# Issuing a second pass's gathers behind the third feed-forward pair's weight sums, and one weight product in another place, on one core

## The chip, the cores and the metric

One core of one Trainium2 chip runs the whole program. The metric is the device time of one execution in microseconds (us); lower is better. The engines are called PE (TensorE matmul), PEld (its weight loads), DVE (VectorE), ACT (ScalarE), POOL (GpSimd) and SP (SyncE).

## The reference

The input x has 32 sequences of 64 tokens, 1024 wide, in float32. One transformer block is computed:

- a linear layer with a low-rank addition chosen by a label for each sequence (`x @ W.T + 0.5 * (x @ A[label]) @ B.T`, rank 32, 5 labels),
- attention on its result (32 query heads, 8 key and value heads, rotary embedding, causal softmax, output projection), added to x,
- a linear layer with a mixture of 8 low-rank experts (top 2 after a bias for the language of the sequence),
- a feed-forward linear layer with a second mixture of 8 low-rank experts, whose result is added again.

No nonlinear function stands between the first linear layer and the query, key and value projection, nor between the third and the fourth layer. The kernel therefore multiplies the weights of such neighbours with each other first.

## The kernel before

**Stages.** Stage 1 multiplies weights: `cq` (first layer by the query and key columns), `ckv` (by the rest of the keys and the values) and `cf` (third layer by fourth). Their results go to scratch in HBM (`cqkv`, `cffn`, `wos`). Stage 2 is run twice, for `hf` 0 and 1, each with 16 of the 32 sequences: low-rank rows, query and key products (`qk_pair`), scores, softmax, values, output projection (`o_pairs`), router gates, and four feed-forward pairs (`ffn_pair(0)` to `ffn_pair(3)`, called f00 to f03 in the first pass below).

**Seven products in place of eight.** Every large product is cut into 2 by 2 blocks and done with seven block products and some sums (class `Group`). Its steps `p1` to `p7` are block products of 4 chunks each; they accumulate in three PSUM banks x, y and z:

- x takes `p1`, and then `p2` on top; `out00` reads it.
- y takes `p6`, then `p7`, then `p4`. Between them DVE reads it: after `p6` for `add01` (line 285, tile `cq_u` or `f_u`), after `p7` for `add11` (line 297), after `p4` for `out10`.
- z takes `p5`, then `p3`. Between them `out11` reads it, which needs `add11` too; after `p3`, `out01` reads it.

A later step of a bank waits on PE until the earlier reader is through. The banks come from `group_bank`, three in turn, so that the sixth bank taken is the third one again, once it has been read.

**Weight sums.** `weight_sums` makes four 128x512 sums of a weight tile on POOL (lines 176 to 179). Tiles `w` and `s` have two buffers each, so the sums of the third pair wait until the first pair's last product with a sum, `p3`, is done.

**Stage 1 order.** SP, PE and DVE follow the order written in the code. For `cq` the first two groups are interleaved by hand, in the list `order` of the call of `multiply`; a step `(1, "p5")` is `p5` of group 1.

**First feed-forward pair.** Its main products run before its gates are there (`without_extra`). Then `scaled` turns the gates round on PE (`gpr`), copies them on ACT (`gsr`) and multiplies on DVE (`hwr`), and `with_extra` adds the expert terms (line 270) to z, x and y, calls `out11` and `out00`, and goes on with `p3` and `out10`. The other pairs use `Group.main`, with the expert terms as a fifth chunk of each product (`tail`, line 265).

**Gathers.** For each sequence `gathered` issues one indirect DMA on POOL's queue, which fetches 128 rows of the label's low-rank factor. For the first pass they are issued in stage 1, in two lots of eight. For the second pass all 16 go into a part of tile `q`, and the place in POOL's queue is set by hand:

```python
with tc.issue_after(late["gates"].ins):
    tiles = [
        gathered(hf, s, lambda name: a1[:, s * BS : (s + 1) * BS], BS) for s in range(NS)
    ]
```

`late["gates"]` is the last copy made by `gates_of`, on POOL at line 756: at that point the first pass's second gates. The gathered rows are first used by `first_halves`, at the head of the second pass's PE work.

Of the kernel before, what the change touches and what calls it, by code (L numbers as in the profile page):

```python
# [13 lines left out]
F32 = mybir.dt.float32  # L14
# [5 lines left out]
P = 128  # L20
D = 1024
KC = D // P
# [3 lines left out]
E, R = 8, 16  # L26
# [3 lines left out]
NT = TH // P  # L30
# [46 lines left out]
def block_kernel(ctx: ExitStack, tc: tile.TileContext, a, out: bass.AP):  # L77
    nc = tc.nc
    PSUM = bass.MemoryType.PSUM

    const = ctx.enter_context(tc.tile_pool(name="const", bufs=1))
# [13 lines left out]
    def tmp(name):  # L95
        return tp.tile([P, 512], F32, tag="t", name=name)

    def small(name):
        return sm.tile([P, NT, E], F32, tag="small", name=name, bufs=12)


    cst = const.tile([P, NCONST], F32, tag="consts", name="consts")
    ident, parts = cst[:, _C["ident"]], cst[:, _C["parts"]]
    stack = cst[:, _C["stack"]]
# [64 lines left out]
    def weight_sums(w, name, s=None):  # L169

        h = w.shape[1] // 2
        a11, a12 = w[:, :h, :P], w[:, h:, :P]
        a21, a22 = w[:, :h, P:], w[:, h:, P:]
        if s is None:
            s = wp.tile([P, 4, h, P], F32, tag="s", name=f"s_{name}")
        nc.gpsimd.tensor_add(s[:, 0], a21, a22)  # L176
        nc.gpsimd.tensor_sub(s[:, 1], s[:, 0], a11)
        nc.gpsimd.tensor_sub(s[:, 2], a11, a21)
        nc.gpsimd.tensor_sub(s[:, 3], a12, s[:, 1])
        return s  # L180

    def column_sums(t, b, cols, which=range(4)):
# [216 lines left out]
    def load_w(from_, name):  # L399
        w = wp.tile([P, KC, WG], F32, tag="w", name=f"w_{name}")  # L400
        nc.sync.dma_start(w, from_)
        return w
# [6 lines left out]
    def gathered(hf, s, new, n):  # L409

        tiles = []
        for b0 in range(0, BS, n):
            t = new(f"a1_{hf}_{s}_{b0}")
            for b in range(n):
                at = hf * BH + s * BS + b0 + b
                nc.gpsimd.indirect_dma_start(
                    t[:, b, :],
                    None,
                    a["a1"],
                    bass.IndirectOffsetOnAxis(ap=rows_of[:, at : at + 1], axis=0),  # L420
                )
            tiles.append(t)
        return tiles

    def ranks(hf, s, x, tiles, low):

        n = BS // len(tiles)
        ps = ps_tile(f"h_{hf}_{s}")
        rows = tmp(f"rows_{hf}_{s}")

        def half(i):
            for b in range(BS):
                for g in range(4):
                    kc = i * 4 + g
                    nc.tensor.matmul(
                        ps[g * LR : (g + 1) * LR, b * S : (b + 1) * S],
                        tiles[b // n][:, b % n, kc * LR : (kc + 1) * LR],
                        x[kc][:, (s * BS + b) * S : (s * BS + b + 1) * S],

                        start=(i, b) == (0, 0),  # L440
                        stop=i == 1,
                        skip_group_check=True,
                    )
            if i == 1:

                nc.scalar.mul(rows, ps, 0.5)

        def stacked():
            ps = ps_tile(f"low_{hf}_{s}")
            nc.tensor.matmul(ps, stack, rows, start=True, stop=True)  # L450
            nc.scalar.copy(low[:, s * 512 : (s + 1) * 512], ps)

        return lambda: half(0), lambda: half(1), stacked

    def new_low(hf):
        return hp.tile([P, TH], F32, tag="hw", name=f"low_{hf}")
# [22 lines left out]
    with tc.tile_pool(name="gen", bufs=1) as gen:  # L479
# [146 lines left out]
        def load_kv(w):  # L626
# [4 lines left out]
            "cq", "w1", t_cq, D, cqkv, 0, first=(w0, w1),  # L631
            order=[
                *((0, "p1"), (1, "p1"), (0, "p2"), (1, "p2"), (0, "p6"), (0, "p5"), (0, "p7"), (1, "p6")),
                *((0, "out11"), (0, "p4"), (0, "p3"), (1, "p5"), (1, "p7"), (1, "out11"), (1, "p4"), (1, "p3")),
            ],
            after={
                (0, "p1"): lambda w: b1q_rows[0](),
# [63 lines left out]
        )  # L701


    late = {"logits": const.tile([P, KC, 32], F32, tag="wr", name="wr")}
    nc.sync.dma_start(late["logits"], a["wr2"])
    in_order.close()

# [3 lines left out]
    def gates_of(n, hf, lgv, more):  # L711


        nm = f"r{n}_{hf}"

        def wide(v):
            return v.unsqueeze(2).to_broadcast([P, NT, E])

        def one(name):
            return sm.tile([P, NT], F32, tag="one", name=f"{name}{nm}", bufs=10)  # L720

        em = em8.unsqueeze(1).to_broadcast([P, NT, E])
        l1 = small(f"l1{nm}")
        nc.vector.tensor_add(l1, lgv, more)

        def first_max(lv, k):

            m = one(f"m{k}")
            nc.vector.tensor_reduce(m, lv, AX.X, ALU.max)
            eq = small(f"eq{k}{nm}")  # L730
            nc.vector.tensor_tensor(eq, lv, wide(m), ALU.is_equal)
            nc.vector.tensor_mul(eq, eq, em)
            i = one(f"i{k}")
            nc.vector.tensor_reduce(i, eq, AX.X, ALU.min)
            oh = small(f"oh{k}{nm}")
            nc.vector.tensor_tensor(oh, em, wide(i), ALU.is_equal)
            return m, oh

        m1, oh1 = first_max(l1, 1)
        l2 = small(f"l2{nm}")  # L740
        nc.vector.scalar_tensor_tensor(l2, oh1, -3e38, l1, ALU.mult, ALU.add)
        m2, oh2 = first_max(l2, 2)

        e = one("e")
        nc.vector.tensor_sub(e, m2, m1)
        nc.scalar.activation(e, e, AF.Exp)
        g1 = one("g1")
        nc.vector.tensor_scalar(g1, e, 0.5, 0.5, ALU.mult, ALU.add)
        nc.vector.reciprocal(g1, g1)
        g2 = one("g2")  # L750
        nc.vector.tensor_mul(g2, g1, e)
        nc.vector.tensor_mul(oh1, oh1, wide(g1))
        nc.vector.tensor_mul(oh2, oh2, wide(g2))
        nc.vector.tensor_add(oh1, oh1, oh2)
        gates = late["pool"].tile([P, NT, E, R], F32, tag="gates", name=f"gates{nm}")
        late["gates"] = nc.gpsimd.tensor_copy(gates, oh1.unsqueeze(3).to_broadcast([P, NT, E, R]))
        return gates

    def scaled(n, hf, h, gates):
# [17 lines left out]
    def scoped(name, bufs=1, side="left"):  # L777
        return pools.enter_context(tc.tile_pool(name=name, bufs=bufs, side=side, reuse_waits="tile"))

    for hf in range(2):  # L780
# [13 lines left out]
        if hf == 0:  # L794
            low = first_pass["low"]
        else:

            low = new_low(hf)
            a1 = q[:, 1].rearrange("p b m t -> p b (m t)")
            with tc.issue_after(late["gates"].ins):  # L800
                tiles = [
                    gathered(hf, s, lambda name: a1[:, s * BS : (s + 1) * BS], BS) for s in range(NS)
                ]
            steps = [ranks(hf, s, x, tiles[s], low) for s in range(NS)]
            first_halves, second_halves, sums = zip(*steps)
# [248 lines left out]
        with tc.manual_schedule():  # L1054
# [3 lines left out]
            for u in range(2):  # L1058
                g = pair
# [26 lines left out]
            sums = scoped(f"sums_o{hf}")  # L1086
# [141 lines left out]
        def ffn_pair(g):  # L1228
            w = load_w(cffn[:, :, g * WG : (g + 1) * WG], f"f{hf}{g}")

            def out_f(r, c, ps, add):
                oc = 2 * g + r
                o = tmp(f"o_{hf}_{oc}_{c}")
                if add is None:
                    nc.scalar.activation(o, ps, AF.Identity, bias=bb[:, oc : oc + 1])
                else:
                    nc.vector.scalar_tensor_tensor(o, ps, bb[:, oc : oc + 1], add, ALU.add, ALU.add)  # L1237
                nc.scalar.dma_start(out[oc, :, hf, c, :], o)

            def extra(r, c):  # L1240
                if (r, c) == (0, 1):
                    return [(bd[:, 0], hw2[1]), (bd[:, 1], hw3[1])]
                return [(b2v[:, 0, r], hw2[c]), (b3v[:, 0, r], hw3[c])]

            def tail(left, right):
                lhs = {"11": b2v[:, g, 0], "12": b3v[:, g, 0], "22": b3v[:, g, 1]}
                rhs = {"11": hw2[0], "21": hw3[0], "22": hw3[1]}
                return (
                    bs[:, int(left[1]) - 1, g - 1] if left[0] == "s" else lhs[left],
                    th[:, int(right[1]) - 1] if right[0] == "t" else rhs[right],  # L1250
                )

            s = weight_sums(w, f"f{hf}{g}")
            if g == 0:
                return Group(f"f{hf}{g}", w, s, xt, out_f, extra, late=True)
            group = Group(f"f{hf}{g}", w, s, xt, out_f)
            group.tail = tail
            return group
# [19 lines left out]
        first.with_extra()  # L1278
        column_sums([th[:, j] for j in range(4)], lambda i, c: (hw2, hw3)[i][c], lambda t: t)
        for g in range(1, 4):  # L1280
            ffn_pair(g).main()
        pools.close()


# [86 lines left out]
```

## Time and profile before

| | |
|---|---|
| median of 3 runs | 1216.33 us (1215.64 to 1218.25) |
| the profiled execution's own time | 1218.22 us |
| its span, first to last instruction | 1216.5 us, granted TensorE clock 0.998 |
| PE busy | 1204.8 us (99%) |
| DVE, POOL, ACT busy | 582.2, 509.6, 153.6 us |
| DMA | 108.83 MB, mean 89 GB/s |
| the second pass's 16 gathers on POOL | from 633.83 to 654.11 us |
| second pass's first use of the gathered rows | 753.25 us |

Times in the views are us from the span's start. A timeline row has start, duration, engine, line, operation, tiles and count; in brackets stands the idle time of the engine before it, and what ended it. "remote" there means that a semaphore moved which the profile can lay to no instruction that had just ended. A row of the view by stretches has the stretch, its length, the busy time of PE, PEld, DVE, ACT and POOL with the number of instructions, the granted PE clock, the DMA engines' busy share and GB/s.

### The profile page before, as it was taken

To read this page: it belongs to the slowest core of one execution; us is meant where nothing else is said; L and a number is where in the kernel's file an instruction comes from. 1 tells how busy PE (TensorE), PEld (TensorE's weight loads), DVE (VectorE), ACT (ScalarE), POOL (GpSimd) and SP (SyncE) were. 2 spreads that over 40 slices of the span, in tenths; PEclk is the share of its full clock that TensorE was granted. 3 is DMA by queue.
4 is the path that set the end of the run, shared out by engine and by line. 5 is a ranking of instruction groups with operands and counts; after the bars stand their busy time and mean duration, and the time that the engine had idled before them with its cause. 6 is when DMAs were issued, how large, how long until landed. Compare 5 with 4: busy or idle time off the path is not lost.

```text
span 1216.5 us, 13619 instructions
## 1 busy us (share of the span) xinstructions
PE 1204.8 (99%) x5440; PEld 612.9 (50%) x5440; DVE 582.2 (48%) x941; ACT 153.6 (13%) x282; POOL 509.6 (42%) x437
## 2 busy tenths in 40 slices
PE   9999999999999999999998999999999999999998
PEld 3444875555444477544443444444468544444443
DVE  5212161115358789764832113456789764842111
ACT  1001000000001125320000000100214330000000
POOL 3441351443435746745635011542756653821010
PEclk9999999999999999999999999999999999999999
DMA  6653732644111111122114225111120123112110
GB/s 243 222 205 110 273 120 81 205 146 153 35 34 36 43 62 71 43 74 96 35 47 126 69 85 192 36 35 35 36 70 17 55 70 116 60 35 69 57 48 34
DMA packets 58992, 108.83 MB, mean 89 GB/s; under 512 B 5168, under 2 KB 35248, under 8 KB 57648
## 3 DMA queue, kind: packets, MB, share of 16 engines
q1 hardware_dynamic: 43136, 79.53, 19.7%
q10 hardware_dynamic: 13104, 20.03, 4.5%
q0 software_dynamic: 2688, 8.39, 2.1%
q8 instruction: 43, 0.70, 0.3%
q14 instruction: 21, 0.17, 0.0%
HBM read 83.72 MB, written 24.22 MB: 89 GB/s over the span
## 4 chain that ended last, share of the span: by engine, by line
PE 97%; DMA 1%; DVE 0%; another core or an unknown queue 0%; SPq 0%; ACT 0%; issue 0%; DVEq 0%; ACTq 0%
PE qk_y L255 9%; PE o_y L255 7%; PE f_y L255 7%; PE qk_x L255 6%; PE qk_z L255 6%; PE v L873 5%; PE f_z L255 5%; PE o_x L255 5%; PE f_x L255 5%; PE o_z L255 5%; PE cq_y L255 3%; PE cf_y L255 3%; PE sc L894 3%; PE pt L947 2%; PE cf_z L255 2%; PE cq_z L255 2%
## 5 line engine op out<-in xcount | busy, mean ns | idle before, releaser
L823 POOL TENSOR_TENSOR raw<-raw,consts 128x512 f32<-128x512 f32 x40 | 63.1, 1586 | 105.8 <-DVE t L822 105.8
L927 POOL TENSOR_TENSOR e<-e,top 128x512 f32<-128x512 f32 x64 | 65.0, 1045 | 57.3 <-DVE top L926 42.2
L939 POOL TENSOR_TENSOR e<-e,tot 128x512 f32<-128x512 f32 x64 | 66.2, 1067 | 27.2 <-DVE tot L937 27.2
L255 PE MATMUL qk_x<-x,w_qk 128*128 128x512 f32 x160 | 72.2, 594 | 0.0
L255 PE MATMUL qk_y<-sum_x,s_qk 128*128 128x512 f32 x160 | 72.2, 594 | 0.0
L176 POOL TENSOR_TENSOR s_f<-w_f 128x512 f32<-128x512 f32 x8 | 11.0, 1370 | 127.6 <-DMA w_f<-cffn 99.7
L255 PE MATMUL o_x<-q,w_o 128*128 128x512 f32 x128 | 58.9, 592 | 0.0
L873 PE MATMUL v<-w_v,x 128*128 128x256 f32 x256 | 58.7, 382 | 0.0
L255 PE MATMUL f_x<-x,w_f 128*128 128x512 f32 x128 | 57.9, 592 | 0.0
L255 PE MATMUL f_y<-sum_y,s_f 128*128 128x512 f32 x128 | 57.5, 592 | 0.0
L1048 POOL TENSOR_TENSOR x<-x,o_u 128x512 f32<-128x512 f32 x24 | 31.0, 1294 | 54.2 <-DVE o_u L1046 33.2
L873 PEld LDWEIGHTS v<-w_v,x 128*128 128x128 f32 x256 | 47.4, 190 | 8.4 <-issue 2.7
L255 PEld LDWEIGHTS qk_x<-x,w_qk 128*128 128x128 f32 x160 | 30.1, 190 | 38.0 <-issue 37.9
L824 DVE TENSOR_TENSOR t<-t,consts 128x512 f32<-128x512 f32 x40 | 48.7, 1230 | 0.7
L255 PEld LDWEIGHTS qk_y<-sum_x,s_qk 128*128 128x128 f32 x160 | 30.2, 190 | 37.1 <-issue 36.6
L176 POOL TENSOR_TENSOR s_qk<-w_qk 128x512 f32<-128x512 f32 x10 | 19.1, 1906 | 65.8 <-DMA w_qk<-cqkv 65.8
L936 DVE TENSOR_REDUCE tot<-e 128x8 f32<-128x512 f32 x64 | 40.5, 666 | 10.7 <-ACT e L931 10.4
L931 ACT ACTIVATE e<-e 128x512 f32<-128x512 f32 x64 | 38.2, 639 | 54.3 <-POOL e L927 54.2
L917 DVE TENSOR_TENSOR e<-sc,consts 128x512 f32<-128x512 f32 x64 | 39.7, 676 | 8.8 <-PE sc L894 8.8
L1237 DVE SCALAR_TENSOR_TENSOR o<-f_z,consts,f_u 128x512 f32<-128x512 f32 x16 | 12.0, 751 | 58.6 <-PE f_z L265 42.6
L255 PEld LDWEIGHTS f_y<-sum_y,s_f 128*128 128x128 f32 x128 | 24.3, 190 | 30.6 <-issue 30.6
L255 PEld LDWEIGHTS f_x<-x,w_f 128*128 128x128 f32 x128 | 24.3, 190 | 30.6 <-issue 30.6
(321 smaller groups left out, 2239.3 us busy)
## 6 DMA issues: line engine op xcount, KB each, us to landing
w_qk<-cqkv SPq DMA_DIRECT2D x10, 1024.0 KB, 6.2
x<-in_xT SPq DMA_DIRECT2D x16, 512.0 KB, 8.1
w_o<-in_wo SPq DMA_DIRECT2D x16, 512.0 KB, 4.9
s_o<-wos SPq DMA_DIRECT2D x16, 512.0 KB, 6.7
w_f<-cffn SPq DMA_DIRECT2D x8, 1024.0 KB, 5.4
outT<-o ACTq DMA_DIRECT2D x32, 256.0 KB, 2.8
cqkv<-cq ACTq DMA_DIRECT2D x16, 256.0 KB, 2.3
w_ckv<-in_w SPq DMA_DIRECT2D x4, 1024.0 KB, 6.6
```

The costliest lines, as they stand in the source:

```text
L176: nc.gpsimd.tensor_add(s[:, 0], a21, a22)
L255: nc.tensor.matmul(ps, self.weights[left][:, kc, :], self.right(right, kc), start=first and kc == 0, stop=kc == self.h - 1, skip_group_che ...
L823: nc.gpsimd.tensor_mul(rv, rv, c3)
L824: nc.vector.tensor_mul(t2v, t2v, s3)
L873: nc.tensor.matmul(begun[t], x[kc][:, t * P : (t + 1) * P], wv[:, kc, :], start=False, stop=kc == KC - 1, skip_group_check=True,)
L894: nc.tensor.matmul(sc[j][:, n * S : (n + 1) * S], q[rows, g, b, 2 * mp : 2 * mp + 2, :].rearrange("p m t -> p (m t)"), k[rows, g, b, :], s ...
L917: nc.vector.tensor_add(per_key(e), per_key(sc[j]), mask.unsqueeze(1).to_broadcast([P, 8, S]))
L927: nc.gpsimd.tensor_sub(ev, ev, wide(top))
L931: nc.scalar.activation(e, e, AF.Exp, scale=SCALE)
L936: nc.vector.tensor_reduce(tot[:, i], es[i], AX.X, ALU.add)
L939: nc.gpsimd.tensor_mul(es[i], es[i], wide(tot[:, i]))
L1048: nc.gpsimd.tensor_add(xo, xo, to)
```

## The change

Two edits. In the first, each call of `weight_sums` keeps its last instruction in `late["sums"]`, the one of the third pair (`g == 2`) is kept as `late["third"]`, and the second pass's gathers are issued after it; nothing is kept of the gates any more. POOL's queue then holds the second gates' copy, the four sums `s_f02`, the 16 gathers, the four sums `s_f03`; before it held the copy, the gathers, `s_f02`, `s_f03`. In the second, `(0, "p3")` of the `cq` list moves from behind `(0, "p4")` to behind `(1, "p7")`. The queue orders of the two programs differ in these places alone: PE's by the moved product; DVE's by the exchange of the two additions that follow `(0, "p3")` and `(1, "p7")`; in ACT's and SP's queues the instructions keep their order, but DMAs around the place use and wait for other slots (x1 to x6 of the eight loads of x among them).

```diff
+    late = {}
@@ weight_sums
-        nc.gpsimd.tensor_sub(s[:, 3], a12, s[:, 1])
+        late["sums"] = nc.gpsimd.tensor_sub(s[:, 3], a12, s[:, 1])
@@ multiply("cq", ...)
             order=[
                 *((0, "p1"), (1, "p1"), (0, "p2"), (1, "p2"), (0, "p6"), (0, "p5"), (0, "p7"), (1, "p6")),
-                *((0, "out11"), (0, "p4"), (0, "p3"), (1, "p5"), (1, "p7"), (1, "out11"), (1, "p4"), (1, "p3")),
+                *((0, "out11"), (0, "p4"), (1, "p5"), (1, "p7"), (0, "p3"), (1, "out11"), (1, "p4"), (1, "p3")),
             ],
@@
-    late = {"logits": const.tile([P, KC, 32], F32, tag="wr", name="wr")}
+    late["logits"] = const.tile([P, KC, 32], F32, tag="wr", name="wr")
@@ gates_of
-        late["gates"] = nc.gpsimd.tensor_copy(gates, oh1.unsqueeze(3).to_broadcast([P, NT, E, R]))
+        nc.gpsimd.tensor_copy(gates, oh1.unsqueeze(3).to_broadcast([P, NT, E, R]))
@@ second pass
-            with tc.issue_after(late["gates"].ins):
+            with tc.issue_after(late["third"].ins):
@@ the pass's last pairs
         for g in range(1, 4):
-            ffn_pair(g).main()
+            group = ffn_pair(g)
+            if g == 2:
+                late["third"] = late["sums"]
+            group.main()
```

## The prediction

> **What bounds the kernel now.** I read the page first. PE is busy for 99% of the span, and the clock row is full. So time can only be won where PE idles or runs slowly; other engines matter where PE waits for them.
>
> ```profile
> PE 1204.8 (99%) x5440; PEld 612.9 (50%) x5440; DVE 582.2 (48%) x941; ACT 153.6 (13%) x282; POOL 509.6 (42%) x437
> PE   9999999999999999999998999999999999999998
> ```
>
> The one inner slice below 9 is the 22nd, about 639 to 669 us. The view of waits, for PE alone, says what ended its idle time:
>
> ```profile
> PE f_z L255 <- DVE o L1237: 3.0, 1, 3.0
> ...
> PE f_z L270 <- DVE hwr L774: 1.2, 1, 1.2
> PE cq_y L255 <- DVE cq_u L297: 0.8, 1, 0.8
> ```
>
> The third is what the second edit concerns. The first two lie in the first pass's first feed-forward pair, beside the gathers. The second pass runs the same instructions without gathers, so it is a control. Measured from `h_x` (600.70 and 1065.50) the passes are 464.80 us apart, and still so at the gates' turning (645.57 and 1110.37). From there, in the timeline of PE:
>
> ```profile
> 649.50 1.12 PE L270 MATMUL f_z<-hwr,b 128*128 128x512 f32 x2 [1.18 <-DVE hwr L774]
> ...
> 655.33 5.29 PE L255 MATMUL f_z<-x,s_f 128*128 128x512 f32 x8 [2.99 <-DVE o L1237]
> ...
> 663.03 3.60 PE L255 MATMUL f_x<-x,w_f 128*128 128x512 f32 x8
> ...
> 1113.03 1.12 PE L270 MATMUL f_z<-hwr,b 128*128 128x512 f32 x2
> ...
> 1115.71 3.61 PE L255 MATMUL f_z<-x,s_f 128*128 128x512 f32 x8
> ...
> 1121.74 3.60 PE L255 MATMUL f_x<-x,w_f 128*128 128x512 f32 x8
> ```
>
> At the next pair the distance is 1121.74 - 663.03 = 458.71 us: the first pass lost **6.09 us** within 18 us. Three pieces: 1.27 us by 649.50, 3.15 more by 655.33, and 1.67 because the next product took 5.29 in place of 3.61 us. By stretches (the clock is the figure after the five engines, the DMA share the next):
>
> ```profile
> 645.57:654.10 8.53, 5.60 (x19) 2.50 (x17) 3.28 (x5) 1.17 (x2) 6.70 (x7) 1.00 0.75 229
> ...
> 1110.37:1118.90 8.53, 8.53 (x27) 4.11 (x26) 3.85 (x6) 1.76 (x3) 0.00 (x0) 1.00 0.61 184
> ...
> 655.20:658.50 3.30, 3.17 (x4) 1.51 (x5) 0.08 (x1) 0.69 (x1) 0.00 (x0) 0.50 0.27 99
> ```
>
> The granted clock is halved after the idle 3 us. The DMA share is 0.61 without harm in the second pass, so load alone is not the cause; POOL is the difference, 6.70 against 0. What PE waited for was itself late:
>
> ```profile
> 654.52 0.75 DVE L1237 SCALAR_TENSOR_TENSOR o<-f_z,consts,f_u 128x512 f32<-128x512 f32 x1 [3.15 <-remote]
> ...
> 656.70 0.69 ACT L1235 ACTIVATE o<-f_x,consts 128x512 f32<-128x512 f32 x1 [7.98 <-remote]
> ...
> 80.38 0.60 ACT L446 ACTIVATE rows<-h 128x512 f32<-128x512 f32 x1 [13.57 <-remote]
> ...
> 1115.11 0.69 ACT L1235 ACTIVATE o<-f_x,consts 128x512 f32<-128x512 f32 x1 [2.97 <-PE f_x L270]
> ```
>
> Both read a bank that PE had filled. From the filling product's start, DVE began 654.52 - 649.50 = 5.02 us later, against 1.80 in the second pass (late by 3.2); ACT 6.24 against 1.12 (late by 5.1). "remote" stands only four times in the whole trace: these three and the `gsr` copy at 648.14 (late by about 1.4). All fall in or within 3 us of a stretch of gathers (78.26 to 88.00, 633.83 to 654.11). So I read: **while gathers are issued, some of PE's completion signals arrive 1.4 to 5.1 us late.** Not all: four handovers were late, and six prompt (DVE at 638.90, ACT at 646.26 and 82.07, and DVE at 37.65, 41.15 and 44.51, the last three at the first lot of gathers).
>
> [...] I infer the link from place and time. [...]
>
> **The change part by part.** *Gathers.* Nothing is added or removed; 16 instructions of 0.95 us with 0.30 between (20.3 us in all) move behind four sums of 1.27. `s_f02` gains nothing by going first: it began at 660.71, released by PE's `f_z`, 6.6 us after the last gather. Without the loss it starts as in the second pass, 1119.41 - 464.80 = 654.6, and ends at 659.7. Gathers then run from 659.7 to about 680.0. Behind them POOL holds `s_f03`, begun at 698.36 on a DMA, so at 692.3: 12 us spare. The gathered rows are first read at 753.25 - 6.1 = 747: over 60 us spare. SP's `w_f02` load now runs without them.
>
> What else stands in 659.7 to 682? The second pair, f01. Its handovers from the timeline of before: DVE's `u1` ends at 672.58, `p7` starts at 675.91 (slack 3.3); `out11` ends at 681.88, `p3` starts at 684.49 (slack 2.6); later ones over 3. In f00 that last slack was 0.14 (DVE's `o` ends 1115.57, PE starts 1115.71). A late signal costs what exceeds the slack: at 3.2 us 0.6, at 5.1 us 2.5, plus up to 1.7 if the clock falls. Four of ten signals were late, and only two here meet a small slack; I take 0.3 us (bounds 0 and 4.2). Removed: 6.1 (bounds 0, were it chance, and 6.1).
>
> *cq.* Now PE stands 0.84 us before `(1, "p4")`, since DVE reads bank y for 0.69 us after `(1, "p7")`. The moved product (8 instructions, 3.43 us from its start to the next one's) covers that. But its old cover goes too: it stood between `(0, "p4")` and `(1, "p5")`, and the latter takes the sixth bank, which is group 0's y. `out10` reads that at 44.51 to 45.20, where PE would start at 44.31. Same handover, same 0.84 us, moved from 54.8 to 44.5. Net **0** (bounds -0.3 and +0.5 for what I mis-see of starts overlapping). `s_cq2` waits for the moved product, so about 55.7 in place of 50.23 to start; its 5.1 us end at 60.8, needed at 66.02. `out11` of group 1 stands behind another DVE addition; two take 1.4 us under a 3.4 us product. The ACT and SP slots: the x loads landed for 76.41 without a PE wait, `w_cq3` at 72.7 for 89.60; a us more is hidden.
>
> *Sum.* The profiled execution took 1218.22 us (span 1216.5 and 1.7 around). 1218.22 - 6.1 + 0.3 + 0 = 1212.4. It is 1.89 above the median of the three, and they spread over 2.6. If that spread is the late signals' own variation, the median holds 4.2 of the loss and ends at the same 1212.4; if it is anything else, 1216.33 - 5.8 = 1210.5. I take the middle, **1211.5 us**.
>
> **Rivals.** (a) *The lateness goes with the gathers and bites in f01.* For: nothing ties it to f00. Against: slack 2.6 and 3.3 in place of 0.14. At the largest lateness once, 2.5 + 1.7 comes back: 1216.33 - 6.1 + 4.2 = 1214.4, within 0.2% (2.4 us, about what a measurement here can tell). (b) *The loss was chance in the profiled execution, or the change misses it.* Then 1216.3. Against: the other runs would be near 1212 unless they carry most of it. (c) *Slower: late signals at both of f01's handovers, with the halved clock each time.* From a lateness of 6.6 us on, idle is 3.3 and 4.0 and the halved clock adds 3.4: 10.7 - 6.1 gives +4.6, 1220.9. [...] Against: 5.1 was the most seen.
>
> **How the numbers follow.** Forecast 0.73, (a) 0.13, (b) 0.09, (c) 0.05. Half of (a) is milder and still faster, and a little of the forecast is mild too: faster 0.79, same 0.15, slower 0.06. The range, 1209.7 to 1215.0, reaches from the full loss taken off the median, less 0.5 for cq, over 1212.4 to (a); what is left out is (b), (c) and the tail of (a).
>
> **What would show it.** In the timeline after: no PE gap before `f_z` L270 and L255 in f00, the product there at 3.6 us, and a distance of 464.8 between the passes at `f_x` of f01; gathers from about 660 to 680, `s_f03` not moved by them. In PE's waits the cq row names `cq_z` with L550, still 0.8. Any "remote" should now be in f01, without a PE gap over 1 us. Wrong: "remote" waits in f00 without gathers near, or a PE gap over 3 us in f01.

## The result, and the profile after

| | before | after |
|---|---|---|
| median of 13 runs, on one chip | 1217.46 us (1213.88 to 1218.54) | 1213.27 us (1211.69 to 1214.77) |
| ratio, with its 95% interval | | 0.9972 (0.9963 to 0.998) |
| the profiled execution | 1218.22 us, span 1216.5 | 1213.1 us, span 1211.3 |

The range after leaves one run out, 1237.45 us under a granted clock of 0.973. The changed kernel is faster by 3.4 us by the ratio (2.4 to 4.5 by its interval) and by 4.2 by the medians; 1211.5 was forecast. Lines of the code are 3 higher than before.

The page shows PE at the same 99%, and the 22nd slice is full:

```profile
PE 1203.2 (99%) x5440; PEld 611.9 (51%) x5440; DVE 577.9 (48%) x941; ACT 153.4 (13%) x282; POOL 511.4 (42%) x437
...
PE   9999999999999999999999999999999999999998
```

In PE's waits (total, times, longest, in us) both rows of `f_z` are gone. The row of `cq` is there at the same size, under the other name:

```profile
PE idle L134 <- DVE idle L131: 1.5, 1, 1.5
PE cq_z L258 <- DVE cq L553: 0.8, 1, 0.8
PE cq_x L258 <- DMA wq<-in_wqkv: 0.7, 3, 0.4
```

The timeline of PE, first pass and then second, at the place that lost 6.09 us:

```profile
646.65 1.04 PE L770 MATMUL gpr<-consts,gatesr 128*128 128x128 f32 x8
...
649.31 1.12 PE L273 MATMUL f_z<-hwr,b 128*128 128x512 f32 x2
...
651.99 3.61 PE L258 MATMUL f_z<-x,s_f 128*128 128x512 f32 x8
...
658.01 3.60 PE L258 MATMUL f_x<-x,w_f 128*128 128x512 f32 x8
...
1105.25 1.04 PE L770 MATMUL gpr<-consts,gatesr 128*128 128x128 f32 x8
...
1110.58 3.61 PE L258 MATMUL f_z<-x,s_f 128*128 128x512 f32 x8
```

No bracket stands behind a row: PE waits for nothing. From `gpr` to `f_x` of the next pair it takes 658.01 - 646.65 = 11.36 us; before it took 663.03 - 645.57 = 17.46. This distance, **`gpr` to `f_x`**, is the measure of the loss in all that follows; 11.36 means none. By stretches the first pass's row is now the second pass's of before, POOL's 0.00 included, and the clock stays at 1.00:

```profile
646.65:655.18 8.53, 8.53 (x27) 4.11 (x26) 3.85 (x6) 1.76 (x3) 0.00 (x0) 1.00 0.57 184
655.18:658.02 2.84, 2.84 (x8) 1.17 (x8) 0.66 (x1) 0.00 (x0) 2.33 (x2) 1.00 0.00 0
```

One late handover is left beside the moved gathers (660.90 to 680.71), in f01 and on ACT:

```profile
681.99 0.69 ACT L1238 ACTIVATE o<-f_x,consts 128x512 f32<-128x512 f32 x1 [18.90 <-remote]
```

The product that fills its bank ended at 679.63 on PE, and the reader began 2.4 us after that (in the second pass 0.04). It is through at 682.68, and PE takes that bank again at 688.05: 5.4 us of slack, and nothing waits. The copy `rows` of stage 1, whose gathers were not moved, is late as before.

### The profile page after: what moved, and what is told of

Same layout as the page of the kernel before. It is cut to its first block, busy times and chain, and to the rows that moved or that the text cites. A ratio compares the mean times of both kernels' runs of the same rounds, so it can differ in the third digit from the quotient of the medians.

```text
span 1211.3 us, 13619 instructions
## 1 busy us (share of the span) xinstructions
PE 1203.2 (99%) x5440; PEld 611.9 (51%) x5440; DVE 577.9 (48%) x941; ACT 153.4 (13%) x282; POOL 511.4 (42%) x437
## 4 chain that ended last, share of the span: by engine, by line
PE 98%; DMA 1%; SPq 0%; DVE 0%; issue 0%
PE qk_y L258 9%; PE o_y L258 7%; PE f_y L258 7%; PE qk_x L258 6%; PE qk_z L258 6%; PE v L876 5%; PE f_z L258 5%; PE o_x L258 5%; PE f_x L258 5%; PE o_z L258 5%; PE cq_y L258 3%; PE cf_y L258 3%; PE sc L897 3%; PE pt L950 2%; PE cq_z L258 2%; PE cf_z L258 2%
## 5 line engine op out<-in xcount | busy, mean ns | idle before, releaser
L836 DVE TENSOR_TENSOR q<-raw,t 128x512 f32<-128x512 f32 x32 | 38.4, 1205 | 2.5 <-POOL raw L826 2.3
```

Source lines behind the costliest of these rows:

```text
L836: nc.vector.tensor_add(*unfinished.pop())
```

## The experiments

The experiments ran in five series on five chips, B to F; the chip of the first comparison is called A (it may be one of them). Each series ran the kernel before as well, but no trace of it was taken there. **Theory**: gathers on POOL make PE's completion signals late, and f00 has no slack for it. **Rivals**: it was chance or belongs to the place; the `cq` order brought the gain; it is the DMA traffic of the rows, not their issue.

**First series, chip B.** The two edits apart (each kernel takes one edit of the diff shown above and leaves the other as before).

> The changed kernel with the old cq order: the gathers' edit alone. If the gain is all from the gathers (my theory), the time is that of the changed kernel, 3.4 us +/- 1 below the kernel before, and PE's wait stands before cq_y again, 0.8 us. If the cq edit brought part of the gain, it is missing here: 0.5 to 3 us slower than the changed kernel.

> The kernel before with the new cq order: the other edit alone. Theory (the stall of 0.84 us only moves): as the kernel before within 0.5 us, the wait now before cq_z (line 255). If it brings something, 0.5 to 3 us faster than before. It is also a second look at the gathers in their old place: theory, late signals ('remote') at f00's handovers again and a distance gpr to f_x near 14 to 17.5 us; if the loss was chance in one execution, 11.4 us.

| chip B | median us | ratio to before |
|---|---|---|
| before (41 runs) | 1213.14 | |
| gathers' edit alone | 1213.32 | 1.0001 (0.9993 to 1.001) |
| `cq` edit alone | 1213.13 | 0.9998 (0.999 to 1.0006) |

Neither did anything, since on this chip **the kernel before doesn't lose the time**: it takes 1213.14 us. With the gathers at their old place, the second kernel takes 657.42 - 646.06 = 11.36 us from `gpr` to `f_x`:

```profile
646.06 1.04 PE L767 MATMUL gpr<-consts,gatesr 128*128 128x128 f32 x8
...
657.42 3.60 PE L255 MATMUL f_x<-x,w_f 128*128 128x512 f32 x8
```

Both expectations for the gathers failed, that of a gain and that of late signals at their old place. The one for `cq` held: the time is the same, and the wait stood before `cq_z`, 0.79 us.

The third kernel brings the gathers back beside a pair, in the second pass:

```diff
+        if hf == 1:
+            spare = scoped("spare").tile([P, 2, BS, KC * LR], F32, tag="spare", name="spare")
+            with tc.issue_after(late["gates"].ins):
+                for s in range(NS):
+                    gathered(hf, s, lambda name: spare[:, s], BS)
```

> The changed kernel with 16 more gathers (the same rows, into a spare tile that nothing reads) in the second pass, behind its second gates on POOL, the place where the first pass had them before. My theory (gathers make PE's completion signals late, f00 has 0.14 us of slack): the second pass's f00 loses 1 to 6 us, with 'remote' at its handovers, gpr to f_x 13 to 17.5 us in place of 11.4, and the time is about 2.5 to 6 us above the changed kernel. Rival, chance or something in the first pass alone: 11.4 us, and the time as the changed kernel within 0.5 us.

1212.89 us, ratio 0.9999 (0.9991 to 1.0007), and 1115.86 - 1104.49 = 11.37 us in the second pass: as the rival said. The stretch shows that the load was really there, POOL at 6.70 us as in the kernel before and DMA at 0.80:

```profile
1104.45:1112.98 8.53, 8.53 (x27) 4.07 (x26) 3.85 (x6) 1.76 (x3) 6.70 (x7) 1.00 0.80 266
```

So gathers alone don't make signals late on this chip. A difference between the chips can be seen in every trace at one place, the copy `rows` on ACT near 80 us, which reads a bank of PE beside the first pass's gathers. On chip A, changed kernel, and on chip B, gathers' edit alone:

```profile
81.44 0.60 ACT L449 ACTIVATE rows<-h 128x512 f32<-128x512 f32 x1 [13.53 <-remote]
```

```profile
79.16 0.60 ACT L449 ACTIVATE rows<-h 128x512 f32<-128x512 f32 x1 [11.81 <-PE h L438]
```

ACT idles 13.5 us for it on the one and 11.8 on the other. I take this as the **mark** of a chip with late signals. Theory, second form: on a chip with the mark, gathers make signals late.

**Second series, chip C (mark: 13.56, "remote").** The same program as the last, and a delay made by hand.

> Once more the changed kernel with 16 more gathers behind the second pass's second gates, since on the chip of the first comparison no kernel showed late signals, the kernel before among them (1213.14 us). If this chip shows them in the kernel before (its time then about 1217): theory, the second pass's f00 loses 1 to 6 us with 'remote' at its handovers and the time is near that of the kernel before; rival (not the gathers), 11.4 us from gpr to f_x and about 1213. If the kernel before is at 1213 here too, lateness belongs to a state of the chip, and both are at 1213.

The kernel before took 1218.58 us (1215.95 to 1222.92), this one 1217.80, ratio 0.9996 (0.9984 to 1.0009), as expected: what the changed kernel won on chip A isn't there. The first pass is clean (657.29 - 645.93 = 11.36). In the second, from the timelines of PE, then DVE, then ACT:

```profile
1104.45 1.04 PE L770 MATMUL gpr<-consts,gatesr 128*128 128x128 f32 x8
...
1108.38 1.13 PE L273 MATMUL f_z<-hwr,b 128*128 128x512 f32 x2 [1.17 <-DVE hwr L777]
...
1114.20 3.70 PE L258 MATMUL f_z<-x,s_f 128*128 128x512 f32 x8 [2.98 <-DVE o L1240]
...
1120.31 3.60 PE L258 MATMUL f_x<-x,w_f 128*128 128x512 f32 x8
```

```profile
1113.40 0.75 DVE L1240 SCALAR_TENSOR_TENSOR o<-f_z,consts,f_u 128x512 f32<-128x512 f32 x1 [3.15 <-remote]
```

```profile
1115.58 0.69 ACT L1238 ACTIVATE o<-f_x,consts 128x512 f32<-128x512 f32 x1 [7.98 <-remote]
```

These are the numbers of the first pass of the kernel before on chip A, in another series and in the other pass: PE's gaps are 1.17 and 2.98 (before: 1.18 and 2.99), and DVE's idle time of 3.15 and ACT's of 7.98 are the same to the hundredth. With the gathers the loss has moved to the other pass; it is neither chance nor tied to the first pass. From `gpr` to `f_x`: 1120.31 - 1104.45 = 15.86, a loss of 4.50. It is not 6.09, since the clock didn't fall: the product took 3.70 us.

The second kernel makes the delay without late signals:

```diff
+                    for _ in range({(0, 0): 5, (0, 1): 6, (1, 0): 6}.get((hf, g), 0) if r * c else 0):
+                        nc.vector.tensor_copy(o, ps)
                     nc.vector.scalar_tensor_tensor(o, ps, bb[:, oc : oc + 1], add, ALU.add, ALU.add)
```

DVE copies the bank 5 or 6 times before `out11` reads it. PE's order is held by hand but for the terms that move ahead of the delayed product: in f00 one of `f_y`, in the first pass's f01 the first two instructions of f02's `p1`.

> The changed kernel with out11 made late by hand, the late signal's stand-in: DVE copies the bank 5, 6 and 6 times (about 0.68 us each) ahead of out11 in the first pass's f00, the first pass's f01 and the second pass's f00; PE has one expert term (0.86 us) in f00, two terms' time of f_x in f01 to go on with. Theory (a late handover costs what exceeds the slack, 0.14 us in f00 and 2.6 in f01, and an idle of about 3 us halves the clock for 3.4 us, 1.7 us more): PE gaps of 2.4, 0.6 and 3.1 us, the product behind the third 5.3 us and perhaps behind the first; 6 to 9.5 us slower than the changed kernel. Rival (the stall is mostly taken up by later slack on PE): under 3 us slower.

The clock's figures in it are those of the kernel before: behind its gap of 2.99 us the clock was 0.50 for 3.41 us (655.16 to 658.57), and the product took 5.29 us in place of 3.61. Measured here: 1227.22 us, ratio 1.0062 (1.0037 to 1.0086) to the kernel before. That is 14 us above the changed kernel, which ran on chip A only, where 6 to 9.5 were expected. PE's three gaps:

```profile
655.00 3.70 PE L258 MATMUL f_z<-x,s_f 128*128 128x512 f32 x8 [2.52 <-DVE o L1248]
...
686.10 3.78 PE L258 MATMUL f_x<-x,w_f 128*128 128x512 f32 x4 [4.22 <-ACT o L1244]
...
1123.83 5.40 PE L258 MATMUL f_z<-x,s_f 128*128 128x512 f32 x8 [3.25 <-DVE o L1248]
```

The gaps in f00 are close to what was computed (2.4 and 3.1), and f00 lost 7.98 us in the two passes together. Behind the first the clock stays; behind the third it is halved for 3.41 us, and behind the second for 6.82 (stretches of this run, clock in the figure after the five engines):

```profile
655.00:658.50 3.50, 3.50 (x8) 1.63 (x9) 0.00 (x0) 0.00 (x0) 0.00 (x0) 1.00 0.20 75
684.47:691.29 6.82, 5.19 (x6) 2.19 (x7) 0.00 (x0) 0.69 (x1) 0.00 (x0) 0.50 0.28 96
1124.79:1128.20 3.41, 3.41 (x6) 1.32 (x5) 0.00 (x0) 0.00 (x0) 0.00 (x0) 0.50 0.17 64
```

The second gap, 4.22 us where 0.6 was expected, makes the excess. PE didn't wait there for the delayed DVE but for ACT:

```profile
680.86 1.02 PE L268 MATMUL f_x<-hwr,b 128*128 128x512 f32 x2
```

```profile
685.36 0.69 ACT L1244 ACTIVATE o<-f_x,consts 128x512 f32<-128x512 f32 x1 [20.03 <-issue]
```

ACT began 3.5 us after that product had ended on PE (681.88); gathers ran to 683.89. ("issue" means that the profile shows nothing that ACT waited for.) It is the handover that was late in the changed kernel too; there PE came back to the bank 5.4 us later, here f02's first product had been pulled forward and met it. Together the three places lost 2.78 + 6.72 + 5.20 = 14.7 us against the changed kernel: the first and third by `gpr` to `f_x`, the second as what else lengthens the way from the first pass's `gpr` to the second's. The spans differ by 1225.5 - 1211.3 = 14.2. So a late reader costs what exceeds its slack, but PE's order decides how much slack there is.

**Third series, chip D (mark: 13.58 to 13.59).** Which part of a gather does it? Both kernels are the kernel before with another form of the 16 loads.

```diff
+                if hf == 1:
+                    nc.gpsimd.dma_start(t[:, b, :], a["a1"][:P])
+                    continue
```

> The kernel before with the second pass's 16 gathers turned into plain DMAs of fixed rows on POOL's queue, in the same order and place (left out: the choice of the rows by label in the second pass). On a chip where the kernel before is at about 1217: if issuing any DMA of this kind on POOL makes PE's signals late, the same loss as before, gpr to f_x of f01 14 to 17.5 us in the first pass; if it needs the indirect form (its longer work on POOL, its reading of the row numbers), 11.4 us and about 1213. On a chip where the kernel before is at 1213, no difference is expected of either.

1213.24 us beside 1217.71, ratio 0.9963 (0.9951 to 0.9975), and 657.27 - 645.91 = 11.36. But POOL issued the 16 within 8.52 us and was through at 642.5, before `gpr` and so before each of the handovers of f00 that were late:

```profile
633.96 8.52 POOL L417 DMA_DIRECT2D q<-in_a  x16
```

So it shows that the loss goes when nothing is issued there, not that the plain form is harmless.

In the other, the loads go through SP behind the load of `w_f02` (`loads` keeps the instruction of each weight load), at the time of the handovers:

```diff
+                if hf == 1:
+                    nc.sync.dma_start(t[:, b, :], a["a1"][:P])
+                    continue
...
-            with tc.issue_after(late["gates"].ins):
+            with tc.issue_after(loads["f02"].ins):
```

> The kernel before with those 16 loads as plain DMAs on SP's queue, behind the load w_f02, so that they run beside f00 as the gathers did (left out: the choice of the rows by label in the second pass). If the lateness comes from issuing on POOL: no late signal in f00, gpr to f_x 11.4 us, and 4 us faster than the kernel before where that is at 1217. If it comes from the DMA traffic of these rows, the loss stays, 14 to 17.5 us.

1212.93 us, ratio 0.9961 (0.9948 to 0.9975); 657.31 - 645.95 = 11.36. The timeline of PE stands first, then the stretch from `gpr` on. The stretch holds more DMA traffic than that of the kernel before on chip A (0.88 against 0.75), POOL does nothing in it, and PE is full:

```profile
645.95 1.04 PE L772 MATMUL gpr<-consts,gatesr 128*128 128x128 f32 x8
...
657.31 3.60 PE L255 MATMUL f_x<-x,w_f 128*128 128x512 f32 x8
```

```profile
645.95:654.48 8.53, 8.53 (x27) 4.11 (x26) 3.85 (x6) 1.76 (x3) 0.00 (x0) 1.00 0.88 270
```

SP issued the 16 from 646.80 to 658.33. So the amount of traffic is ruled out as the cause. This kernel has the old `cq` order, and it is 4.8 us faster than the kernel before: the gain isn't from `cq`.

**One more line, to beat both.** The `cq` wait that the change only moved comes from the bank. One more line takes it away: z of group 1 comes from the pool of `ps_tile`, so that `(1, "p5")` needn't wait until DVE has read y of group 0.

```diff
-            self.z = self.bank("z")
+            self.z = (self.z_new or self.new)(f"{self.name}_z")[:, : self.n]
@@ multiply, groups in a written order
+                    if order is not None and g == 1:
+                        groups[g].z_new = ps_tile
```

> The changed kernel, but the sixth bank of cq (z of group 1) comes from another pool of banks, so that (1, p5) need not wait until DVE has read group 0's y. Theory: the wait of 0.8 us before cq_z goes and nothing takes its place, so 0.8 us faster than the changed kernel. Rival: PE is handed on to the next wait (the reader of (1, p7), or the weight's load), and the time stays as that of the changed kernel.

> The changed kernel with cq's sixth bank from another pool, once more, as the version to beat both: it measured 1212.22 us where the changed kernel's like (gathers alone) measured 1213.32. Expected 0.8 to 1.1 us below the changed kernel again; against the kernel before, about 1 us less where that is at 1213, and about 5 us less where it is at 1217 (signals that are late beside the gathers meet slack).

On chip B it took 1212.22 us, 0.9994 (0.9986 to 1.0003) of the kernel before, which isn't clear of the spread. Its median is 1.1 us under that of the gathers' edit alone, and 9 of its 13 runs are below the lowest of that kernel's (1212.59). On chip D it took 1211.93, **0.9947 (0.9925 to 0.9968)** of the kernel before, 5.8 us less. The changed kernel itself was run on neither chip. The timeline of PE on chip D shows the product without a wait:

```profile
41.68 3.60 PE L259 MATMUL cq_y<-sum_cq,w_cq 128*128 128x512 f32 x8
45.12 3.60 PE L259 MATMUL cq_z<-sum_cq,s_cq 128*128 128x512 f32 x8
```

3.44 us lie between the two starts, in the changed kernel 46.42 - 42.05 = 4.37.

**Fourth and fifth series, chips E and F (no mark: 11.77 and 11.76).** The open question of the form, with the columns in thirds so that POOL issues past the handovers, and the gathers' edit alone again.

```diff
+                if hf == 1:
+                    for cols in (slice(0, 96), slice(96, 176), slice(176, 256)):
+                        nc.gpsimd.dma_start(t[:, b, cols], a["a1"][:P, cols])
+                    continue
```

> The kernel before with the second pass's 16 gathers turned into 48 plain DMAs on POOL's queue, each a third of the columns of fixed rows (left out: the choice of the rows by label in the second pass). 16 plain ones took only 8.5 us and were through by 642.5 us, before the handovers of f00; 48 at 0.53 us run to about 659 and stand beside all of them. On a chip where the kernel before is at about 1217.5: if any DMA issued on POOL makes PE's signals late, gpr to f_x is 13 to 17.5 us in the first pass and the time 1215 to 1218; if only the indirect form does, 11.4 us and about 1213.

> Once more the changed kernel with the old cq order, the gathers' edit alone. On a chip where the kernel before is at about 1217.5: theory, the whole gain, 3.5 to 5 us faster than before, no PE gap in f00. If part of the gain came from the cq order, less than 3 us. On a chip where the kernel before is at 1213: no difference, as measured.

> The 48 plain DMAs on POOL's queue once more (left out: the choice of the rows by label in the second pass), for a chip that shows late signals; the mark of one is the copy 'rows' on ACT, near 80 us, ended by 'remote'. With that mark: if any DMA issued on POOL makes PE's signals late, gpr to f_x is 13 to 17.5 us in the first pass and the time 1215 to 1218; if only the indirect form does, 11.4 us and about 1213 beside a kernel before of about 1217.5. Without the mark nothing is told.

On E the kernel before took 1213.32, the thirds 1213.26 (ratio 1.0001, 0.9992 to 1.0009) and the gathers' edit 1213.26 (1.0004, 0.9995 to 1.0013); on F 1213.39 and 1213.22 (1.0, 0.9991 to 1.0009). Chips without the mark tell nothing of the form, so it stays **open** whether a plain DMA issued on POOL would make signals late too. The gathers' edit alone was not run on a chip with the mark either.

What the series say together:

| chip | `rows` on ACT idles | before, median us | gathers away from f00, us |
|---|---|---|---|
| A | 13.53, remote | 1217.46 | 1213.27 (the change) |
| C | 13.56, remote | 1218.58 | not run |
| D | 13.58, remote | 1217.71 | 1212.93 (loads through SP) |
| B | 11.81, PE | 1213.14 | 1213.32 (gathers' edit) |
| E | 11.77, PE | 1213.32 | 1213.26 (gathers' edit) |
| F | 11.76, PE | 1213.39 | not run |

Where no gathers stand beside f00 (A, B, D, E), the kernel takes 1212 to 1213 us, and the kernel before took about 1218 with the mark and 1213 without it. The change as a whole ran on A alone. Whether the mark belongs to the chip or to the hour can't be told from one series on each.

## Why the prediction was right, step by step

**Where PE loses time**: right. The three pieces in f00 are gone, 17.46 - 11.36 = 6.10 us where 6.1 was put, and no other gap took their place. One number of "What would show it" was wrong: with the loss gone the passes stand 1116.61 - 658.01 = 458.60 us apart, at `gpr` and `f_x` alike, and not 464.8. The 464.8 held the loss of the first pass, which pushed the second one back. The forecast time didn't use it.

**The cause**: right as far as it went, by place and time, and the runs confirm it: gathers moved into the second pass bring the same delays there (chip C, `gpr` to `f_x` 15.86 us), rows loaded through SP at the same time bring none (chip D, 11.36). That it is PE's signal that comes late stays inferred, since "remote" names no instruction. For it speaks that the same program has no such wait on B, and that in the kernel before two handovers from other engines, beside the same gathers, were prompt: ACT's `gsr` ended at 648.73 and DVE began at 648.75, DVE's `hwr` ended at 649.44 and PE began at 649.50. What the prediction could not see from one trace is that the lateness shows only on some chips; on B the very same gathers delayed nothing. It judged chance at 0.09 on the ground that other runs would show it; in three series of six the kernel before took 1213 us and had nothing to lose. That a gain was measured at all was so in part luck: it needed a chip with late signals, like that of the first trace.

**Gathers**: right. The work of the profiled execution ran 1.08 us later throughout (`gpr` 646.65 against 645.57), because the first products of `cq`, which wait for loads, were late by that much before 20 us; where the wait falls differs from run to run. Less that, `s_f02` starts at 654.60 (654.6 was forecast), the gathers run from 659.82 to 679.63 (659.7 to about 680.0), `s_f03` starts at 692.29 on its load (692.3).

**f01**: right in its outcome. The lateness went along with the gathers, as rival (a) said, but met ACT's handover with 5.4 us of slack; the two DVE handovers for which a cost was figured were prompt. Cost 0 where 0.3 was taken. Which handover would be late was not forecast, and how late it is varies: on chip C it was 0.5 us in the kernel with extra gathers and 3.5 with the delay by hand, on chip D 4.0 with the extra bank (the product ended at 678.23, ACT read from 682.22 to 682.91, PE took the bank again at 686.65). One size was too small: DVE's lateness of 3.2 us was counted from when DVE was free; from the end of the filling product (650.62) to 654.52 it is 3.9, which would have cost 1.3 at `out11` of f01 and not 0.6. The delay by hand shows how thin the slack is: with f02's first product pulled forward, ACT's handover cost 4.22 us and a halved clock.

**`cq`**: right. The stall moved from before `(1, "p4")` to before `(1, "p5")`, 0.78 in place of 0.84, and the edit alone measured 0.9998.

**Sum**: 1212.4 was forecast for the profiled execution and 1213.1 measured: 1.1 of the later start, less the 0.3 not paid in f01. Of the two readings of the median, "the spread is the late signals' own variation" was the better one: on the chips without the mark the runs of each kernel lie within about 3 us (but for one run of each of two kernels on B), with it those of the kernel before spread over 4.66, 6.97 and 7.35. The medians of 13 differ by 4.2 us, not by 5.8, and the middle, 1211.5, was 1.8 too low; part of that is the starting point, since the three runs had a median 1.1 below that of the 13. The term that was counted too firmly is the clock's 1.67: on chip C the same two delays left the clock alone and cost 4.50. Of the 38 runs of the kernel before on C and D, 19 had a mean clock of 0.998 or less, with medians of 1219.40 and 1219.30 us; the other 19 had 1216.45 and 1216.55. So it seems that the clock's part is paid in some executions and not in others; the last section shows what went before a fall.

## To carry to other kernels

A wait whose releaser had long been done, named "remote" or late against the same instruction in another pass, is worth more than a row of the waits (here DVE idled 3.15 us and ACT 7.98, and PE lost 6.1): look what POOL issues at that moment, and whether another stage with slack could hold it. Compare both kernels on more than one chip before believing a gain of 0.3%: here it was 0.28% on one chip and, for the edit that matters, nothing on two others, and a mark in the trace told which kind of chip it was. A stall that is only moved is paid at its new place (0.84 us became 0.78); ask which bank or buffer makes it, since one from another pool took it away (3.44 us between two starts in place of 4.37). And see in a trace whether the clock fell behind a gap of PE, before a second cost goes into a sum: behind the gap of 2.99 us it did and the product took 5.29 us, behind that of 2.98 it didn't and the product took 3.70.

## What the runs showed of the hardware

- Readers of PE's banks began late beside gathers in three series of six, by the same amounts in two series and two passes (DVE's idle 3.15 us, ACT's 7.98). In the other three no trace shows it; of these only B has traces with gathers beside a first pair. Gathers on POOL beside a first pair brought late readers (chip C, DMA share 0.71), loads through SP there did not (chip D, 0.88). That fits a cause on POOL's side; no run here shows the path by which it reaches PE's readers.
- A halved clock is decided by more than the length of the gap: 2.52 and 2.98 us left it alone, with 2.99, 3.25 and 4.22 it was halved, and in the gap of 4.22 it fell when PE had idled for only 2.59 us (681.88 to 684.47). In the traces' records of the clock the changes lie whole multiples of 3.413 us apart. In the kernel before it is full for 648.53 us, half for 3.41 and full again for 556.37 (190, 1 and 163 multiples); in the changed kernel it is full for 1204.91 (353); in the run with the delay it is half for 6.82 and for 3.41, and the two falls are 440.32 apart (2, 1 and 129). The stretches of that length next to a change show what PE did there. The last row is an estimate: its stretch is put ten times 3.413 us before the fall at 684.47.

| stretch of 3.41 us | PE busy in it, us | clock in it | clock in the next |
|---|---|---|---|
| before, 651.75 to 655.16 (gap of 2.99) | 0.59 | 1.00 | 0.50 |
| delay, 681.06 to 684.47 (gap of 4.22, begun) | 0.82 | 1.00 | 0.50 |
| delay, 684.47 to 687.89 (gap of 4.22, ended) | 1.79 | 0.50 | 0.50 |
| delay, 1121.38 to 1124.79 (gap of 3.25) | 0.96 | 1.00 | 0.50 |
| delay, 650.34 to 653.75 (gap of 2.52, begun; estimate) | 2.14 | 1.00 | 1.00 |

Of the gap of 2.99 us, 2.82 lay ahead of the fall (652.34 to 655.16). The clock fell behind stretches with 0.59, 0.82 and 0.96 us of work, and not behind the one with 2.14, if that one is rightly placed. Once halved, it was still at 0.50 behind the stretch with 1.79 us of work, and full behind the next (687.89 to 691.30), in which PE was busy throughout. On C the clock stays at 1.00 on both sides of the gap of 2.98 us, so no change marks a stretch there, and what spared that gap isn't shown.

- Plain DMAs on POOL took 8.52 / 16 = 0.53 us each to issue (chip D), gathers 0.95 and 0.30 between (kernel before).
